# Attention over the sequence: the order of the searches for the largest logits, turned by LEAD and paired by length with the weighing steps

## The chip, the cores and the metric

The kernel runs on one core of one Trainium2 chip. The time is the device time of the whole launch in microseconds; smaller is better. Times before the change: 2765.39, 2770.46 and 2771.39 us, median 2770.46.

## What is computed

One decoder layer on x of shape (4, 1024, 256), everything in float32. Three residual blocks follow each other: a gated state-space scan, an attention over a short context (154 keys), and a block with causal attention over the sequence (1024 tokens, 16 heads of depth 16) followed by a mixture of eight experts of which each token uses two. The change touches only the causal attention:

```python
h = _ln(x, ln1_g, ln1_b)
q, k, v = h @ Wq + bq, h @ Wk + bk, h @ Wv + bv      # 16 heads of 16
scores = einsum('bhqd,bhkd->bhqk', q, k) / hd ** 0.5
scores = where(causal, scores, -inf)
attn = softmax(scores, axis=-1)
o = einsum('bhqk,bhkd->bhqd', attn, v)
a = o @ Wo + bo + x
```

## The kernel before

The attentions run on one core in one program whose order is written out by hand for TensorE, VectorE, ScalarE and GpSimd; only the DMA queue of SyncE is ordered by the framework.

*Layout.* A block is 512 query tokens (BLK), half of a batch. The 16 heads lie in four chunks (NCH = 4) of four heads; in a chunk each head takes 32 partitions (HP), of which 16 hold the head's depth. So a matmul over one head has 32 rows, and the four heads of a chunk lie on the four quarters of the rows. A *unit* is one chunk of one block: 8 units for each batch in the context attention and 8 for each batch in the sequence attention.

*Each unit has two halves.* First, `largest` finds the largest logit of each query, so that it can be subtracted ahead of the exponential. Its jobs put queries on the output partitions and keys on the columns: a job takes one tile j of 128 queries, a stretch of at most 512 keys from s0, and a `pair` of heads (0 or 1: heads 0 and 1 or heads 2 and 3, that is the lower or the upper half of the rows). For the causal attention this is `many` (L749): two matmuls into a PSUM tile `ps_max` (L755), for the stretch that ends at the diagonal an addition of the mask (L760), and a reduction to the negative maximum (L762). For the first block of a batch a unit has 8 jobs, of 128, 256, 384 and 512 keys, two of each. For the second block the queries see 640 to 1024 keys, cut into stretches of at most 512: ten jobs of 512, and two each of 384, 256 and 128; there the maxima of the two stretches go to `mpad` and `twice`.

When all searches of a unit are through, `put` (L764) takes the smaller of the two negative maxima (L766, only in second blocks), turns them with four transposes into the PSUM tile `shift` (L769), and adds them to the queries (L771, `qs`).

Second, `weighing` computes the logits again with keys on the output partitions and queries on the columns, for one tile kt of 128 keys and one pair of heads: two matmuls into `ps_exp` (L819), the exponential on ScalarE into `pt` (L821), and on the diagonal a triangle cut to zero on GpSimd (L825). Tiles of keys beyond the diagonal need fewer queries, so the columns are 512, 384, 256 and 128 for the four tiles of a first block, and 512 five times, then 384, 256 and 128 for the eight tiles of a second block. Each comes twice, for pair 0 and then pair 1. After pair 1, `weigh` (L786) multiplies earlier exponentials with the values (L793, `ps_o`).

*Buffers.* `ps_max` and `ps_exp` share three rotating PSUM tiles of two banks each (pool `a_pss`, tag `sc`). `pt` has five buffers, `mpad` two.

*Order.* The main loop walks over the steps of the weighing, unit by unit. After step k of unit u it runs the search jobs up to `upto`: those of unit u+1 in proportion, and LEAD = 5 jobs more. So the searches of a unit begin five jobs before the weighing of the unit ahead of it begins:

```python
upto.append(min(len(search), near + (far - near) * (k + 1) // n + LEAD))
```

`put` of a unit is called when two jobs of the next unit's searches have been issued. After that the loop takes `weigh` at every second step, and `fill` adds at most one job of other TensorE work per step: projections of coming blocks (`proj`, L702), values (`vals`, L715), transposes (`tp`, L689), the way back of finished attention (`back`, L840; `wo`, L859) and the router (L1061). GpSimd and VectorE do small jobs for these in the same order.

*The lines that the change touches* are the last ones of `largest`, where the jobs of the causal attention are put in a list: sorted by falling length, then by j, with pair 0 and pair 1 of each.

Of the kernel before, what the change touches and what calls it, by code (L numbers as in the profile page):

```python
# [27 lines left out]
LEAD = 5  # L28
# [5 lines left out]
BLK = 512  # L34
# [16 lines left out]
def decoder_layer(ctx: ExitStack, tc: tile.TileContext, out: bass.AP, a: dict):  # L51
# [52 lines left out]
    parts = dram.tile([TOPK * NTOK, D], F32, name="parts")  # L104
# [63 lines left out]
    with ExitStack() as ss:  # L168
# [55 lines left out]
        for lv in range(LV):  # L224
            r, h = slice(lv * 2 * NS, (lv + 1) * 2 * NS), 1 << lv
            for x in range(h):
                n = LC // h
# [340 lines left out]
        ready, jobs = prepare(0)  # L568
        for job in jobs:
            job()  # L570
        for blk in range(nblk):
            work = scan(blk, *ready)
            jobs = []
            if blk + 1 < nblk:
                ready, jobs = prepare(blk + 1)
# [27 lines left out]
    with ExitStack() as ss:  # L603
# [9 lines left out]
        def mm_tile(name):  # L613
            return ps_m.tile([P, BLK], F32, tag="mm", name=name)
# [24 lines left out]
        def turn(which, of_):  # L639
            turns[which] += 1  # L640
            return of_[(turns[which] - 1) % len(of_)]
# [83 lines left out]
        def largest(qT, kT, c, keys, diag, shifted):  # L725


            m = turn("m", mpads)
            n_all = [sum(x for _, x in keys) if diag is None else (diag + j + 1) * P for j in range(NJ)]
            jobs = []  # L730
            twice = small.tile([P, NJ, 4], F32, tag="twice", name="twice") if max(n_all) > BLK else None

            def few(j0, pair):

                n = n_all[j0]
                ps = ps_s.tile([P, 2, BLK], F32, tag="sc", name="ps_max")
                for j in range(j0, j0 + 2):
                    for i in range(2):
                        r = slice((2 * pair + i) * HP, (2 * pair + i + 1) * HP)
                        nc.tensor.matmul(  # L740
                            ps[:, i, (j - j0) * n : (j - j0 + 1) * n], qT[r, j * P : (j + 1) * P], kT[r, c, :n],
                            start=True, stop=True,
                        )
                nc.vector.tensor_reduce(  # L744
                    m[:, j0 : j0 + 2, 2 * pair : 2 * pair + 2, HD].rearrange("p j i -> p i j"),
                    ps[:, :, : 2 * n].rearrange("p i (j n) -> p i j n", n=n), AX.X, ALU.max, negate=True,
                )

            def many(j, s0, pair):  # L749
                n = n_all[j]  # L750
                s1 = min(n, s0 + BLK)
                ps = ps_s.tile([P, 2, BLK], F32, tag="sc", name="ps_max")
                for i in range(2):
                    r = slice((2 * pair + i) * HP, (2 * pair + i + 1) * HP)
                    nc.tensor.matmul(  # L755
                        ps[:, i, : s1 - s0], qT[r, j * P : (j + 1) * P], kT[r, c, s0:s1], start=True, stop=True
                    )
                if s1 == n:
                    x = ps[:, :, s1 - s0 - P : s1 - s0]
                    nc.vector.tensor_add(x, x, mask_qk.unsqueeze(1).to_broadcast([P, 2, P]))  # L760
                to = twice[:, j, 2 * pair : 2 * pair + 2] if s0 else m[:, j, 2 * pair : 2 * pair + 2, HD]
                nc.vector.tensor_reduce(to, ps[:, :, : s1 - s0], AX.X, ALU.max, negate=True)  # L762

            def put():  # L764
                if twice is not None:
                    nc.vector.tensor_tensor(m[:, :, :, HD], m[:, :, :, HD], twice, ALU.min)  # L766
                tp = mm_tile("shift")
                for j in range(NJ):
                    nc.tensor.transpose(tp[:, j * P : (j + 1) * P], m[:, j].rearrange("p g i -> p (g i)"), ident)  # L769
                shifted.append(ap_.tile([P, BLK], F32, tag="qs", name="qs", bufs=2))  # L770
                nc.vector.tensor_add(shifted[0], qT, tp)  # L771

            if diag is None:
                for j0 in range(0, NJ, 2):
                    for pair in (0, 1):
                        jobs.append(lambda j0=j0, pair=pair: few(j0, pair))
            else:
                parts = [(min(n - s0, BLK), j, s0) for j, n in enumerate(n_all) for s0 in range(0, n, BLK)]
                for _, j, s0 in sorted(parts, key=lambda x: (-x[0], x[1])):
                    for pair in (0, 1):  # L780
                        jobs.append(lambda j=j, s0=s0, pair=pair: many(j, s0, pair))
            return jobs, put

        waiting, ahead, behind = [], [], []
# [175 lines left out]
        def context(b):  # L960
# [36 lines left out]
            for half in range(T // BLK):  # L997
# [26 lines left out]
                for c in range(NCH):  # L1024
                    shifted = []
                    grp.units.append((
                        largest(qTs[c], kT, c, keys, None, shifted),
                        weighing(shifted, kT, vs, c, keys, None, oT, after if c == NCH - 1 else []),
                    ))
# [109 lines left out]
        def sequence(b):  # L1139
# [54 lines left out]
            for half, (v, qTs) in enumerate(halves):  # L1194
                blk = b * (T // BLK) + half
                xb = xs[:, blk * NJ : (blk + 1) * NJ, :]
                oT = [ap_.tile([P, BLK], F32, tag="oT", name="oT", bufs=5) for _ in range(NCH)]
                res = lazy(late, [P, 2, BLK], "res")
                after = joined(oT, res) + outputs(lambda: held["f"], res, v)
                after += route(blk, xb, v)  # L1200
                after.append(Job(lambda: reach("routed"), lag=0, mm=False))
                keys = [(x * P, P) for x in range(TB)]
                for c in range(NCH):
                    shifted = []
                    grp.units.append((
                        largest(qTs[c], kT, c, keys, half * NJ, shifted),
                        weighing(shifted, kT, vs, c, keys, half * NJ, oT, after if c == NCH - 1 else []),
                    ))
# [11 lines left out]
        for u, (_, jobs) in enumerate(units):  # L1220
            n, near, far = len(jobs), begins[min(u + 1, len(units))], begins[min(u + 2, len(units))]
# [92 lines left out]
    with ExitStack() as ss:  # L1314
# [50 lines left out]
        many = nc.values_load(flag[0:1, 0:1], min_val=0, max_val=P)  # L1365
        with tc.If(many == 0) as branch:
            with ExitStack() as sb:
# [24 lines left out]
                for n in range(NB):  # L1392
                    e = nc.sync.value_load(tab[0:1, 0, n : n + 1], min_val=0, max_val=E - 1)
                    s0 = nc.sync.value_load(tab[0:1, 1, n : n + 1], min_val=0, max_val=E * NTOK - MB)
# [95 lines left out]
```

## Time and profile before

| what | value |
|---|---|
| median of the timed runs | 2770.46 us |
| the profiled execution, its own time | 2737.4 us |
| its span, first to last instruction | 2735.6 us |
| mean granted TensorE clock | 0.927 |
| TensorE busy | 2423.8 us (89%) |
| VectorE busy | 1340.7 us (49%) |
| ScalarE busy | 1014.5 us (37%) |
| attention over the sequence, first to last weighing | 1116.8 to 2037 us, 920.2 us |
| experts | from about 2075 us on |

The profile is of one execution; its own time lies 33 us below the median of the timed runs. Times of instructions are read from that execution. In the lines of the profile a matmul in float32 counts as two records, since it takes two passes through the array, and a record that is written "32*128 32x512" has 32 rows, 128 columns of weights and streams 512 columns. PE is TensorE, PEld its loading of weights, DVE VectorE, ACT ScalarE, POOL GpSimd, SP SyncE. An arrow at the end of a line names what the idle time ahead of the instruction ended with. The busy time of PE is the time in which at least one matmul runs, whatever part of the array it uses.

### The profile page before, as it was taken

To read this page: it belongs to the slowest core of one execution; us is meant where nothing else is said; L and a number is where in the kernel's file an instruction comes from. 1 tells how busy PE (TensorE), PEld (TensorE's weight loads), DVE (VectorE), ACT (ScalarE), POOL (GpSimd) and SP (SyncE) were. 2 spreads that over 40 slices of the span, in tenths; PEclk is the share of its full clock that TensorE was granted. 3 is DMA by queue.
4 is the path that set the end of the run, shared out by engine and by line. 5 is a ranking of instruction groups with operands and counts; after the bars stand their busy time and mean duration, and the time that the engine had idled before them with its cause. 6 is when DMAs were issued, how large, how long until landed. Compare 5 with 4: busy or idle time off the path is not lost.

```text
span 2735.6 us, 36259 instructions
## 1 busy us (share of the span) xinstructions
PE 2423.8 (89%) x13582; PEld 1419.6 (52%) x13582; DVE 1340.7 (49%) x2718; ACT 1014.5 (37%) x1554; POOL 408.2 (15%) x640
## 2 busy tenths in 40 slices
PE   5999999996799999999999999899876999999990
PEld 2666665654344444433333333333335888888880
DVE  4767766566444345676666586566622111111113
ACT  2444334432355445535533544443331222222220
POOL 1110000000110001211312231231231111111110
PEclk9999999997789899999899998898987999999995
DMA  4596000001000000000001001010005555555545
GB/s 102 111 237 153 0 1 1 1 0 26 19 11 21 20 22 17 16 5 24 28 8 37 24 17 26 16 38 9 17 32 170 182 181 180 187 178 183 174 137 185
DMA packets 143601, 191.10 MB, mean 70 GB/s; under 512 B 34130, under 2 KB 114236, under 8 KB 143420
## 3 DMA queue, kind: packets, MB, share of 16 engines
q1 hardware_dynamic: 121628, 131.42, 15.6%
q0 software_dynamic: 15264, 51.00, 7.2%
q10 hardware_dynamic: 6528, 6.29, 0.7%
q8 instruction: 110, 1.80, 0.3%
q14 instruction: 71, 0.58, 0.1%
HBM read 116.03 MB, written 61.24 MB: 65 GB/s over the span
## 4 chain that ended last, share of the span: by engine, by line
PE 56%; issue 24%; DVE 10%; POOL 4%; ACT 3%; DMA 2%; SPq 1%; POOLq 0%; DVEq 0%; ACTq 0%
PE ps_exp L819 12%; PE ps_o L793 7%; PE ps_max L755 6%; PE proj L702 3%; PE ps_xz L310 3%; PE ps_a L327 3%; POOL parts L1381 3%; PE wo L859 2%; PE tp L689 2%; PE z L441 2%; PE ps_o L548 2%; PE ps_max L740 2%; PE vals L715 2%; PE shift L769 1%; PE tp_wt L419 1%
## 5 line engine op out<-in xcount | busy, mean ns | idle before, releaser
L821 ACT ACTIVATE pt<-ps_exp 128x1024 f32<-128x1024 f32 (+4 forms) x512 | 438.1, 861 | 539.1 <-PE ps_exp L819 443.2
L819 PE MATMUL ps_exp<-qs,kT 32*128 32x512 f32 (+4 forms) x2048 | 510.3, 590 | 6.4 <-DVE twice L762 1.9
L755 PE MATMUL ps_max<-kT,qa 32*128 32x512 f32 (+3 forms) x1536 | 363.9, 564 | 13.3 <-ACT pt L821 4.7
L1306 PE MATMUL ps<-hT,w 128*128 128x256 f32 x1248 | 288.3, 384 | 25.2 <-ACT mid L1307 23.5
L762 DVE TENSOR_REDUCE mpad<-ps_max 128x2 f32<-128x1024 f32 (+3 forms) x256 | 261.2, 1024 | 85.1 <-PE ps_max L755 77.9
L1307 ACT ACTIVATE mid<-ps,bias 128x256 f32<-128x256 f32 x312 | 139.4, 473 | 436.8 <-DMA bias<-b1s 257.3
L1312 PE MATMUL ps<-w,mid 128*128 128x256 f32 x1248 | 287.9, 379 | 0.0
L819 PEld LDWEIGHTS ps_exp<-qs,kT 32*128 32x128 f32 (+1 forms) x2048 | 150.1, 183 | 236.5 <-issue 132.3
L1306 PEld LDWEIGHTS ps<-hT,w 128*128 128x128 f32 x1248 | 232.7, 191 | 74.5 <-ACT mid L1307 38.8
L1312 PEld LDWEIGHTS ps<-w,mid 128*128 128x128 f32 x1248 | 234.2, 190 | 30.3
L793 PE MATMUL ps_o<-pt,vs 128*32 128x512 f32 (+4 forms) x2048 | 247.1, 552 | 1.6 <-ACT oT L801 1.2
L760 DVE TENSOR_TENSOR ps_max<-ps_max,mask_qk 128x256 f32<-128x256 f32 x256 | 109.8, 429 | 156.4 <-PE ps_max L755 96.7
L744 DVE TENSOR_REDUCE mpad<-ps_max 128x4 f32<-128x616 f32 x128 | 101.6, 799 | 169.3 <-PE ps_exp L819 113.2
L825 POOL TENSOR_SCALAR_AFFINE_SELECT pt<-pt 128x256 f32<-128x256 f32 x256 | 104.3, 408 | 511.8 <-ACT pt L821 510.6
L1379 DVE TENSOR_TENSOR y<-ps,last 128x256 f32<-128x256 f32 x78 | 33.1, 425 | 294.7 <-PE ps L1312 294.7
L755 PEld LDWEIGHTS ps_max<-kT,qa 32*128 32x128 f32 x1536 | 124.1, 194 | 72.3 <-ACT pt L821 37.4
L1381 POOL DMA_INDIRECT parts<-y,to x78 | 75.8, 972 | 525.0 <-DVE y L1379 521.1
L310 PE MATMUL ps_xz<-xnT,w_in 128*128 128x512 f32 x256 | 125.0, 605 | 0.6 <-ACT xnT L302 0.6
L327 PE MATMUL ps_a<-w,w_a 128*128 128x512 f32 x256 | 121.1, 615 | 0.0
L1406 DVE CAST to<-xr 128x2 int32<-128x2 f32 x39 | 6.6, 169 | 228.8 <-DMA parts<-y,to 201.6
L793 PEld LDWEIGHTS ps_o<-pt,vs 128*32 128x32 f32 (+1 forms) x2048 | 41.9, 110 | 145.0 <-issue 112.3
L740 PE MATMUL ps_max<-kT,qa 32*128 32x154 f32 x1024 | 110.7, 337 | 4.9 <-DVE mpad L744 3.2
(265 smaller groups left out, 3150.6 us busy)
## 6 DMA issues: line engine op xcount, KB each, us to landing
w<-in_L_ffn_e_w_dram SPq DMA_DIRECT2D x78, 1024.0 KB, 5.9
routed<-zero POOLq DMA_DIRECT2D x16, 2080.0 KB, 64.5
xr<-routed SPq DMA_DIRECT2D x39, 260.0 KB, 4.2
qa<-close SPq DMA_DIRECT2D x256, 32.0 KB, 1.9
last<-in_L_ffn_e_b_dram SPq DMA_DIRECT2D x39, 128.0 KB, 5.2
xs<-in_x_dram SPq DMA_DIRECT2D x4, 1024.0 KB, 8.7
kT<-close SPq DMA_DIRECT2D x128, 32.0 KB, 1.9
plain<-row SPq DMA_DIRECT2D x8, 512.0 KB, 3.1
```

Of the source, the lines that this page charges most:

```text
L310: nc.tensor.matmul(ps, w_in[:, k, c * P : (c + 1) * P], xnT[:, k, :], start=k == 0, stop=k == 1)
L327: nc.tensor.matmul(ps, w_a[:, k, c * P : (c + 1) * P], w[:, k, :], start=k == 0, stop=k == 3)
L740: nc.tensor.matmul(ps[:, i, (j - j0) * n : (j - j0 + 1) * n], qT[r, j * P : (j + 1) * P], kT[r, c, :n], start=True, stop=True,)
L755: nc.tensor.matmul(ps[:, i, : s1 - s0], qT[r, j * P : (j + 1) * P], kT[r, c, s0:s1], start=True, stop=True)
L762: nc.vector.tensor_reduce(to, ps[:, :, : s1 - s0], AX.X, ALU.max, negate=True)
L793: nc.tensor.matmul(o[0][g * HP : (g + 1) * HP, off:], vs[:n, kt, (4 * c + g) * HV : (4 * c + g) * HV + HP], pts[g // 2][:n, g % 2, off:], ...
L819: nc.tensor.matmul(ps[:n, i, off:], kT[r, c, k0 : k0 + n], shifted[0][r, off:], start=True, stop=True)
L821: nc.scalar.activation(pt[:n, :, off:], ps[:n, :, off:], AF.Exp, scale=HD**-0.5)
L1306: nc.tensor.matmul(ps, w1[:, k, f * P : (f + 1) * P], hT[:, k, :], start=k == 0, stop=k == 1)
L1307: nc.scalar.activation(mid[:, f, :], ps, AF.Gelu, bias=bias[:, f : f + 1])
L1312: nc.tensor.matmul(ps, mid[:, f, j * P : (j + 1) * P], w2[:, f, :], start=f == 0, stop=f == FF // P - 1)
L1381: nc.gpsimd.indirect_dma_start(out=parts, out_offset=bass.IndirectOffsetOnAxis(ap=to[:, j : j + 1], axis=0), in_=y[:, j, :], in_offset=Non ...
```

## The change

The list of search jobs of a unit of the causal attention is built in another order. It is still sorted by falling length and then by j, now with pair 1 ahead of pair 0, and then turned in a circle: the job at place i is the one at place i - LEAD of the sorted list. With LEAD = 5 a unit of eight jobs begins with the last five of the sorted list (384, 256, 256, 128, 128), and ends with its first three (512, 512, 384); a unit of sixteen begins with 384, 256, 256, 128, 128 and ends with ten of 512 and one of 384.

```diff
             else:
-                parts = [(min(n - s0, BLK), j, s0) for j, n in enumerate(n_all) for s0 in range(0, n, BLK)]
-                for _, j, s0 in sorted(parts, key=lambda x: (-x[0], x[1])):
-                    for pair in (0, 1):
-                        jobs.append(lambda j=j, s0=s0, pair=pair: many(j, s0, pair))
+
+
+                parts = [(min(n - s0, BLK), j, s0, p) for j, n in enumerate(n_all) for s0 in range(0, n, BLK) for p in (1, 0)]
+                parts.sort(key=lambda x: (-x[0], x[1]))
+                for i in range(len(parts)):
+                    _, j, s0, pair = parts[(i - LEAD) % len(parts)]
+                    jobs.append(lambda j=j, s0=s0, pair=pair: many(j, s0, pair))
             return jobs, put
```

The number of jobs, their contents and the points of the main loop at which they are issued stay as they are. This is how the matmuls stand on TensorE in the built programs, from the start of the weighing of the second unit of the first batch (columns and count of matmuls at the end of a row); lines behind L775 move by three in the changed kernel:

```
before                                        after
L819 ps_exp 128x512 x2                        L822 ps_exp 128x512 x2
L755 ps_max 128x256 x2                        L755 ps_max 128x512 x2
L819 ps_exp 128x512 x2                        L822 ps_exp 128x512 x2
L755 ps_max 128x128 x2                        L755 ps_max 128x512 x2
L793 ps_o 32x128 x4                           L796 ps_o 32x128 x4
L819 ps_exp 128x384 x2                        L822 ps_exp 128x384 x2
L755 ps_max 128x128 x2                        L755 ps_max 128x384 x2
L840 back 128x128 x4                          L843 back 128x128 x4
L819 ps_exp 128x384 x2                        L822 ps_exp 128x384 x2
L755 ps_max 128x512 x2 (next unit's)          L755 ps_max 128x384 x2 (next unit's)
L793 ps_o 32x512 x4                           L796 ps_o 32x512 x4
L819 ps_exp 128x256 x2                        L822 ps_exp 128x256 x2
L755 ps_max 128x512 x2                        L755 ps_max 128x256 x2
L769 shift 128x128 x4                         L769 shift 128x128 x4
L819 ps_exp 128x256 x2                        L822 ps_exp 128x256 x2
L755 ps_max 128x384 x2                        L755 ps_max 128x256 x2
L793 ps_o 32x384 x4                           L796 ps_o 32x384 x4
L819 ps_exp 128x128 x2                        L822 ps_exp 128x128 x2
L755 ps_max 128x384 x2                        L755 ps_max 128x128 x2
```

## Prediction

> **What bounds the kernel now.** I read the page first (busy shares, slices), then the windows of the stage that the change touches, then its timeline on TensorE, the groups by shape, and the waits. Terms: a *unit* is one chunk c of four heads over one half of a batch; E is one weighing step's two ps_exp matmuls, S one search job's two ps_max matmuls, W the four ps_o matmuls. While unit u runs its steps k = 0, 1, ..., the searches of unit u+1 run beside them.
>
> The page and the stage (attention over the sequence, from its first E to its last):
>
> ```profile
> PE 2423.8 (89%) x13582; PEld 1419.6 (52%) x13582; DVE 1340.7 (49%) x2718; ACT 1014.5 (37%) x1554; POOL 408.2 (15%) x640
> ...
> 1116.80:2037.00 920.20, 851.62 (x5502) 341.04 (x5502) 588.45 (x1184) 407.39 (x573) 228.57 (x427) 0.93 0.08 21
> ```
>
> The second line's columns are length, then busy time of PE, PEld, DVE, ACT and POOL, then the clock. PE is busy 852 of 920 us, DVE 588, ACT 407: TensorE is the bound, but a busy PE can hold a short matmul beside a long one. The timeline of PE shows that (start, length):
>
> ```profile
> 1161.87 0.59 PE L819 MATMUL ps_exp<-qs,kT 32*128 32x384 f32 x2
> 1161.88 0.70 PE L755 MATMUL ps_max<-kT,qa 32*128 32x512 f32 x2
> 1162.30 0.49 PE L819 MATMUL ps_exp<-qs,kT 32*128 32x384 f32 x2
> 1162.42 0.59 PE L755 MATMUL ps_max<-kT,qa 32*128 32x512 f32 x2
> 1162.94 1.06 PE L793 MATMUL ps_o<-pt,vs 128*32 128x512 f32 x8
> 1163.94 0.48 PE L819 MATMUL ps_exp<-qs,kT 32*128 32x256 f32 x2
> 1163.95 0.70 PE L755 MATMUL ps_max<-kT,qa 32*128 32x512 f32 x2
> 1164.26 0.38 PE L819 MATMUL ps_exp<-qs,kT 32*128 32x256 f32 x2
> 1164.48 0.59 PE L755 MATMUL ps_max<-kT,qa 32*128 32x512 f32 x2
> 1165.01 0.66 PE L769 MATMUL shift<-ident,mpad 128*128 128x128 f32 x4
> ...
> 1167.45 0.38 PE L819 MATMUL ps_exp<-qs,kT 32*128 32x128 f32 x2
> ...
> 1167.66 0.28 PE L819 MATMUL ps_exp<-qs,kT 32*128 32x128 f32 x2
> ```
>
> E and S start 0.01 us apart, on different quarters of the rows, and run together. Each matmul is two passes; the passes start 0.53 (512 columns), 0.43 (384), 0.32 (256) and 0.21 us (128) apart. So a step takes twice that for the *longer* of its two: 1.07, 0.85, 0.64, 0.42 us; E of 256 beside S of 512 costs 1.07 (1163.94 to 1165.01). W takes 1.00 at 512 columns (1162.94 to 1163.94).
>
> What can hold a step back is in the groups by shape and in this stretch of the timeline:
>
> ```profile
> L762 DVE TENSOR_REDUCE mpad<-ps_max 128x2 f32<-128x1024 f32 x156 | 189.8, 1223 | 81.6 <-PE ps_max L755 77.9 <-PE ps_exp L819 2.5
> L760 DVE TENSOR_TENSOR ps_max<-ps_max,mask_qk 128x256 f32<-128x256 f32 x243 | 104.2, 429 | 151.1 <-PE ps_max L755 95.4 <-PE ps_exp L819 49.2 <-ACT pt L821 3.0
> L821 ACT ACTIVATE pt<-ps_exp 128x1024 f32<-128x1024 f32 x192 | 195.1, 1023 | 198.1 <-PE ps_exp L819 129.7 <-PE ps_max L755 66.6 <-POOL row L1046 1.3
> ...
> 1589.83 0.59 PE L819 MATMUL ps_exp<-qs,kT 32*128 32x384 f32 x2
> ...
> 1590.70 0.91 PE L819 MATMUL ps_exp<-qs,kT 32*128 32x384 f32 x4
> 1590.85 1.67 ACT L821 ACTIVATE pt<-ps_exp 128x768 f32<-128x768 f32 x2 [0.20 <-PE ps_exp L819]
> ...
> 1591.71 1.13 PE L755 MATMUL ps_max<-kT,qa 32*128 32x512 f32 x4
> ```
>
> The third pair of lines: E and S take turns in three PSUM buffers (tag sc), so S of step k+1 needs the buffer that exp of E(k) empties, and E(k+2) the one that DVE empties of S(k). E(2) starts at 1589.83, E(3) at 1590.70, but S(3) only at 1591.71, 1.88 us after E(2). Exp starts 0.17 us after its E is through and lasts 1.02, 0.81, 0.60 or 0.38 us (groups of L821 by shape), so S(k+1) starts no sooner than 2.29, 1.86, 1.44 or 1.00 us after E(k) of 512, 384, 256, 128. Other PE work between k and k+1 (*fill*: transposes 0.59 us, proj, wo, vals, router 1.9 us) hides it.
>
> **The change part by part.** No instruction is added or removed; POOL and ACT keep their orders, SP moves two stores of plain by eight issues or fewer, which nobody waits for. Searches keep their places among steps, W and fill; only their lengths trade places. Before, S at step k was five jobs ahead in a list of falling length, so E 512,512,384,384,256,256,128,128 met S 256,128,128,512,512,384,384,256. Now it meets its own length. S also still sits on the row quarters that E of its step leaves free.
>
> *Ceiling.* Columns of the longer of the two: an 8-step unit beside 8 searches 3456, then 2560; 16 beside 16: 8064, then 6656. A column costs (1.07-0.42)/384 = 1.7 ns. Twelve of each kind: 12 x (896 + 1408) x 1.7 ns = 47 us, if nothing but PE counted. It does not, so I go by pairs of steps (k even, k+1, then W), without fill and W, at full clock.
>
> *16 beside 16 (12 units).* (0,1), (2,3): 512s in both, unchanged. (4,5), (6,7), (8,9): S of the second step was 384, 256, 128 and is 512. Where no long fill stands between, the pair ends at 2.29 plus S: 3.14, 2.93, 2.71 before, 3.36 after. Such pairs in the trace: 7, 5 and 7 of 12. That is +0.13, +0.18, +0.37 per unit. After a long fill, S(k+2) starts 0.22 late (2.29 against 1.07 + 1.00 of W); a short S hid that at k = 6, 8, 10, behind 5, 7, 5 of 12 long fills: +0.31. (10,11): 1.86 + 1.07 becomes 1.86 + 0.85: -0.22. (12,13) holds the shift: S ends at 0.64 instead of 1.07; then mask 0.43, reduce 0.69, min 0.18 and 0.2 of hand-over put the transposes at about 2.15 instead of 2.55, and step 13 is 0.64 instead of 1.07: -0.85. (14,15): E 128 beside S 512 twice, 2.14, becomes 1.42 without fill (1.00 + 0.42) and 0.84 with: -1.1 on average. Sum -1.18; x12 = -14.2 us.
>
> *8 beside 8 (12 units), all masked.* (0,1): 2.71 becomes 3.36 in 4 of 12, with a short fill +0.5 once: +0.25. (2,3): -0.22, but where a long fill before makes S(2) late (5 of 12) +0.17: -0.06. (4,5), with the shift, which here waits for nothing: 2.52 becomes 2.08, -0.45. (6,7): 2.40, 2.07, 1.50 (no, short, long fill; 2, 6, 4 of 12) becomes about 1.56, 0.97, 0.84: -0.91; the 1.56 holds a wait of 0.7 for DVE, whose queue is mask, reduce, mask, reduce with the qs addition (0.68) among them. Sum -1.17. In the first unit of each batch DVE is already about full (1116.8 to 1132.0: 13.2 of 15.2 us), so I count it at nothing: 8 x -1.17 = -9.4 us.
>
> *8 beside 16 (4 units)*: DVE sets the pace with the same work in both, 0. *16 beside 8 (3)*: equal sums, -0.6 in all. *Half clock*: 5 of the 12 (14,15) pairs ran so; a saving doubles there, -3 for what DVE leaves of it. *Against*: DVE's small jobs (bn_stats 0.42, reciprocals, additions) stand ahead of masks that are now waited for sooner: +4.
>
> Total -23 us. The profiled execution took 2737.4 us (span 2735.6), 33 below the median of 2770.46; I subtract the same 23 from the median: 2747.5 us, 0.8%.
>
> **Two rules of the skill against rows.** DVE's rows: a masked search costs 0.43 + 0.43 to 1.22 us plus two hand-overs; a pair of 128s 1.84, against PE's 0.84 and a W of 0.36 to 0.57. The Trainium skill, "TensorEngine Tiling (Array Packing)", PSUM Bottleneck, says that tiling speeds up the matmuls but not the emptying of PSUM, which may become the limit. Taken as the rule, every masked step goes at DVE's pace, the 8-step units win nothing and the 16-step units lose most of (14,15): about -2 us. By the rows DVE was idle 332 of 920 us, and W with a fill of 0.59 to 1.9 us (10 of 12 such pairs) covers most of it; I take the rows.
>
> The clock:
>
> ```profile
> PE shift L769 <- DVE mpad L766: 24.8, 16, 2.0
> ...
> 1526.20:1529.60 3.40, 1.42 (x12) 0.59 (x12) 2.48 (x7) 0.94 (x2) 1.09 (x2) 1.00 0.00 0
> 1529.60:1533.00 3.40, 3.40 (x22) 0.95 (x24) 2.61 (x6) 0.60 (x1) 0.73 (x2) 0.50 0.00 0
> ```
>
> The first line: TensorE waited 1.55 us on average for the min ahead of the shift. The windows: 3.4 us with PE busy for 1.42 were followed by 3.4 us at clock 0.50. The skill's "TensorE: Matmul & The Clock Gate" (Why this matters for your kernels) warns only of idle gaps above about 3 us; by it no clock is at stake, by the row a 2 us wait in a thin stretch can cost 1.7 us. The change leaves that wait near 1.5 us but thins the work round it: bounds 0 and 12 x 1.7 = +20; I take 0, as a wait of 1.42 us at 1257 drew no half clock, and keep +20 for the range.
>
> **The rivals.**
> 1. *DVE's pace* (above): the short steps give nothing back, -2 us, 2768. For: the mask and reduce of short steps take over twice PE's time. Against: fill and W.
> 2. *Slower: long pairs wait for exp.* The long steps that now all stand together pay 0.22 to 0.65 each through the three buffers: +0.99 per 16-step unit, +0.42 per 8-step unit, 12 of each, +17; with half-clock windows as above +8: 2787 to 2796. It decides if the short pairs give back less than 1 and 0.4 us per unit.
> 3. *Nearly the whole ceiling*: fills fall where they hide the waits, -40, 2730.
> 4. *The change doesn't pair equal lengths*: excluded; in the built program E 512 stands before S 512, E 128 before S 128, except beside 8 or 16 unequal steps.
>
> **How the numbers follow.** Forecast 0.62 (own range 2735 to 2762); rival 3 0.14; rival 1 0.10; rival 2 0.14. What a measurement can tell from no change is 0.2%, 5.5 us. Faster: 0.62 + 0.14 + 0.02 of rival 1 = 0.78; same 0.08; slower 0.14. The range leaves out most of rival 2 and the end of rival 3: 2726 to 2775.
>
> **What would show it.** After: pairs (14,15) and (6,7) shorter by about 1 us, 512-512 pairs without fill 3.36; L755's wait for ACT pt (4.7 us in 13 times) grows; the shift's wait stays near 1.5 us each; the stage loses about 23 of 920 us, DVE's busy 588 unchanged. Wrong if pairs of 128 take 1.8 and more, or half clock grows by over 20 us.

## The result, and the profile after

| kernel | timed runs | median us | range us | mean granted clock |
|---|---|---|---|---|
| before (first series) | 4 | 2770.93 | 2765.39 to 2776.06 | |
| changed (first series) | 4 | 2731.41 | 2724.77 to 2733.19 | 0.921 to 0.924 |
| before, once more (second series) | 22 | 2772.14 | 2739.30 to 2782.18 | 0.909 to 0.927 |
| changed, once more (second series) | 6 | 2733.74 | 2732.43 to 2739.24 | 0.920 to 0.923 |

The change makes the kernel faster: ratio 0.9853, 95% interval 0.9828 to 0.9879, some 40 us. In the second series it is 0.9891 (0.9849 to 0.9933), with medians 38 us apart; ratios leave out runs more than 1.5% above the fastest of their kernel, eleven of the 52 runs of the kernel before that this one was taken against, so it gives some 30 us. The forecast was 23 us (2747.5). Its range, 2726 to 2775, holds the 2731.4, but the narrower 2735 to 2762 of the forecast itself does not.

The changed kernel's profiled execution took 2732.85 us. The line of its page, and the whole stage (columns as before the change: length, busy PE, PEld, DVE, ACT, POOL, clock). The window runs from the first E to 20 us behind the last W, as does the window of 920.2 us shown before the change: there the last W ends at 2017.3 and not at 2037.

```profile
PE 2414.8 (88%) x13582; PEld 1431.2 (52%) x13582; DVE 1341.0 (49%) x2718; ACT 1014.7 (37%) x1554; POOL 408.8 (15%) x640
...
1124.90:2032.20 907.30, 833.39 (x5503) 347.80 (x5502) 591.02 (x1183) 407.33 (x573) 228.57 (x427) 0.92 0.08 22
```

Work and instructions are the same, DVE is as busy as before (588 and 591), the stage is 13 us shorter than the 920.2 shown before the change. That is a third of what the timed runs say, so the profile shown there was not a typical one: at 2737 us and clock 0.927 it is at the quick end of what that kernel does. A second trace of it, 2773.02 us at clock 0.913, stands below beside the changed kernel, split at the batches. The kernel before, second trace:

```profile
1123.80:1359.10 235.30, 223.91 (x1371) 88.51 (x1370) 146.93 (x273) 102.70 (x144) 48.24 (x94) 0.88 0.06 17
...
1834.90:2051.80 216.90, 199.08 (x1289) 76.79 (x1286) 132.82 (x273) 89.01 (x122) 53.90 (x105) 0.88 0.05 16
1123.80:2051.80 928.00, 868.62 (x5464) 343.10 (x5464) 582.61 (x1160) 406.01 (x570) 220.19 (x419) 0.90 0.07 20
```

Changed:

```profile
1124.90:1341.00 216.10, 203.88 (x1372) 83.93 (x1371) 146.42 (x273) 102.23 (x144) 48.25 (x94) 0.94 0.07 18
...
1796.10:2011.90 215.80, 196.22 (x1289) 78.05 (x1285) 133.67 (x273) 89.71 (x122) 53.85 (x104) 0.87 0.05 17
1124.90:2011.90 887.00, 821.33 (x5464) 339.87 (x5463) 584.44 (x1158) 405.57 (x570) 219.77 (x418) 0.92 0.07 21
```

Lines are first batch, last batch and all four up to the last W. Against this trace the stage is 41.0 us shorter, and the clock is to be read with it: 0.88 against 0.94 in the first batch. The first trace of before had 219.7 us at 0.95 there. So part of the gain is fewer microseconds at half clock, that is with a granted clock of 0.50 in the clock records; in the stage these records know only 0.50 and full clock.

*How much each part is.* The two traces of the kernel before hold 119.5 and 182.0 us of half clock between the first and the last E and differ by 27.6 us in length: 0.44 us for each microsecond of half clock (an estimate). With that price taken off, and units grouped by what runs beside what (8/16: an eight-step unit beside the sixteen searches of the next unit):

| units | forecast us | before (two traces) | changed | measured us |
|---|---|---|---|---|
| 16/16 (12) | -14.2 | 428.3, 427.9 | 418.5 | -9.6 |
| 8/8, but the first of a batch (8) | -9.4 | 135.6, 135.5 | 127.4 | -8.2 |
| first of a batch (4) | 0 | 61.5, 61.5 | 61.8 | +0.3 |
| 8/16 (4) | 0 | 101.7, 101.8 | 101.0 | -0.8 |
| 16/8 (3), last | -0.6 | 119.2, 119.7 | 118.2 | -1.3 |
| small jobs of DVE | +4 | | in the rows | |
| sum at equal clock | -20.2 | | | -19.6 |
| half clock | -3 | | 133.1 us of it | -21.6 against the second trace, +6.0 against the first |

The timed runs give the same split without any trace. A fit of time against clock over 74 runs of the kernel before and 10 of the changed one puts the changed kernel 19.4 us lower at equal clock (standard error 0.8); at a clock of 0.921 two runs of before took 2751.96 and 2752.68, four of the changed kernel 2732.7 to 2733.3. The remaining 19 us of the 38 between the medians are clock: 0.913 or 0.914 against 0.921.

*The pairs.* The timeline of PE in a masked eight-step unit of the changed kernel (unit 2 of the first batch, counted from 0; start and length):

```profile
1171.55 0.49 PE L822 MATMUL ps_exp<-qs,kT 32*128 32x256 f32 x2
1171.58 0.49 PE L755 MATMUL ps_max<-kT,qa 32*128 32x256 f32 x2
...
1173.63 0.85 PE L796 MATMUL ps_o<-pt,vs 128*32 128x384 f32 x8
1174.42 0.38 PE L822 MATMUL ps_exp<-qs,kT 32*128 32x128 f32 x2
1174.43 0.38 PE L755 MATMUL ps_max<-kT,qa 32*128 32x128 f32 x2
1174.63 0.28 PE L822 MATMUL ps_exp<-qs,kT 32*128 32x128 f32 x2
1174.64 0.28 PE L755 MATMUL ps_max<-kT,qa 32*128 32x128 f32 x2
1174.85 0.66 PE L689 MATMUL tp<-ident,on 128*128 128x128 f32 x4
1175.44 0.38 PE L822 MATMUL ps_exp<-qs,kT 32*128 32x128 f32 x2
```

Equal lengths begin 0.01 to 0.03 us apart, and the matmuls behind them start when both are through; the step of 128 columns takes 0.43 us (1174.42 to 1174.85). Pairs of steps without the time of W and fill, in us at full clock (8/8 with the first units of a batch):

| pair | before | changed | |
|---|---|---|---|
| 16/16 (8,9), no, short, long fill | 2.73, 2.14, 2.12 | 3.37, 2.78, 2.37 | dearer |
| 16/16 (6,7) | 2.94, 2.36, 2.21 | 3.37, 2.78, 2.34 | dearer |
| 16/16 (12,13), with the shift, median | 4.22 | 3.44 | cheaper |
| 16/16 (14,15), no fill, fill | 2.09, 2.14 | 1.45, 0.88 | cheaper |
| 8/8 (0,1), no, short, long fill | 2.73, 2.12, 2.12 | 3.37, 2.63, 2.51 | dearer |
| 8/8 (6,7) | 2.40, 2.07, 1.50 | 1.74, 0.92, 0.91 | cheaper |

The wait views hardly show the dearer pairs: PE's wait at L755 for ACT pt went from 4.7 us in 13 times to

```profile
PE ps_max L755 <- ACT pt L824: 5.9, 16, 0.6
```

They are seen only in the timeline, here a pair (8,9) without fill of the changed kernel:

```profile
1254.50 0.70 PE L822 MATMUL ps_exp<-qs,kT 32*128 32x512 f32 x2
1254.51 0.70 PE L755 MATMUL ps_max<-kT,qa 32*128 32x512 f32 x2
...
1255.47 1.02 PE L822 MATMUL ps_exp<-qs,kT 32*128 32x512 f32 x4
...
1255.73 1.94 ACT L824 ACTIVATE pt<-ps_exp 128x1024 f32<-128x1024 f32 x2 [2.43 <-PE ps_max L755]
...
1256.81 1.13 PE L755 MATMUL ps_max<-kT,qa 32*128 32x512 f32 x4 [0.31 <-ACT pt L824]
```

S(9) starts at 1256.81, 2.31 after E(8), when the first exponential is through. In the meantime E(9) runs alone: the wait turns a shared step into two, and only 0.31 us of it is idle.

### The profile page after: what moved, and what is told of

It reads as the page before. It is cut to its first block, busy times and chain, and to the rows that moved or that the text cites. A ratio compares the mean times of both kernels' runs of the same rounds, so it can differ in the third digit from the quotient of the medians.

```text
span 2731.2 us, 36229 instructions
## 1 busy us (share of the span) xinstructions
PE 2414.8 (88%) x13582; PEld 1431.2 (52%) x13582; DVE 1341.0 (49%) x2718; ACT 1014.7 (37%) x1554; POOL 408.8 (15%) x640
## 4 chain that ended last, share of the span: by engine, by line
PE 55%; issue 23%; DVE 12%; POOL 4%; ACT 3%; DMA 2%; SPq 0%; POOLq 0%; DVEq 0%; ACTq 0%
PE ps_exp L822 13%; PE ps_o L796 7%; PE ps_max L755 4%; PE ps_xz L310 3%; PE proj L702 3%; PE ps_a L327 3%; POOL parts L1384 3%; PE wo L862 2%; PE tp L689 2%; PE z L441 2%; PE ps_max L740 2%; PE ps_o L548 2%; DVE mpad L762 2%; PE shift L769 2%; PE tp_wt L419 1%
## 5 line engine op out<-in xcount | busy, mean ns | idle before, releaser
L822 PE MATMUL ps_exp<-qs,kT 32*128 32x512 f32 (+4 forms) x2048 | 525.5, 604 | 9.4 <-DVE mpad L762 7.3
L755 PE MATMUL ps_max<-kT,qa 32*128 32x512 f32 (+3 forms) x1536 | 361.3, 564 | 8.7 <-ACT pt L824 5.9
L755 PEld LDWEIGHTS ps_max<-kT,qa 32*128 32x128 f32 x1536 | 124.7, 196 | 63.7 <-ACT pt L824 36.2
L327 PE MATMUL ps_a<-w,w_a 128*128 128x512 f32 x256 | 128.6, 648 | 0.0
L740 PE MATMUL ps_max<-kT,qa 32*128 32x154 f32 x1024 | 117.2, 352 | 3.0 <-ACT pt L824 1.2
```

The source lines that it names most:

```text
L327: nc.tensor.matmul(ps, w_a[:, k, c * P : (c + 1) * P], w[:, k, :], start=k == 0, stop=k == 3)
L740: nc.tensor.matmul(ps[:, i, (j - j0) * n : (j - j0 + 1) * n], qT[r, j * P : (j + 1) * P], kT[r, c, :n], start=True, stop=True,)
L755: nc.tensor.matmul(ps[:, i, : s1 - s0], qT[r, j * P : (j + 1) * P], kT[r, c, s0:s1], start=True, stop=True)
L822: nc.tensor.matmul(ps[:n, i, off:], kT[r, c, k0 : k0 + n], shifted[0][r, off:], start=True, stop=True)
```

## The experiments

### Each half of the change alone

Against the changed kernel; the other of the two has 16 in place of 8:

```diff
-                parts.sort(key=lambda x: (-x[0], x[1]))
+                turned = len(parts) == 8
+                parts.sort(key=lambda x: (-x[0], x[1]) if turned else (-x[0], x[1], x[2], x[3]))
...
-                    _, j, s0, pair = parts[(i - LEAD) % len(parts)]
+                    _, j, s0, pair = parts[(i - LEAD) % len(parts) if turned else i]
```

> The kernel before once more, to see how far two series of the same program lie apart and how far one profile lies from the timed runs. Every theory: 0 us, within 0.2% (5.5 us). If the first profile of the kernel before (2737.4 us, 33 us below its median) was only a quick execution, this profile lies nearer 2770 us, and its sequence stage is longer than 920 us; if the profiled execution is always quicker, it lies near 2737 again.

> The changed kernel once more. Theory A (pairs of steps: the long pairs lose 0.2 to 0.7 us each to the wait for the exponential, the short pairs gain 0.4 to 1.1 us): -23 us, and the pairs as in the first profile after. Theory B (nearly the whole ceiling of columns, something else gains too): -40 us, as the first comparison showed. Theory C (the 40 us are partly scatter between executions): between -15 and -30 us.

> Only the units of eight searches are turned and reordered; those of sixteen keep the old order. Theory A: -9 us (8 units at -1.17), at most -14 if the first unit of each batch gains as well. Theory B (columns): 12 x 896 x 1.7 ns = -18 us. Rival 1 (VectorE's pace, since all searches here are masked): 0.

> Only the units of sixteen searches are turned and reordered; those of eight keep the old order. Theory A: -14 us (12 units at -1.18). Theory B (columns): 12 x 1408 x 1.7 ns = -29 us. If the two parts are independent, this and the run with only the units of eight add up to the whole change.

The kernel before against itself: 1.0020 (0.9987 to 1.0052). Its runs lie between 2736 and 2782 us, at clocks from 0.927 down to 0.908, and the first profile was at the quick end. Eight alone: 2755.28 us, 0.9967 (0.9943 to 0.9991); sixteen alone: 2743.40, 0.9921 (0.9892 to 0.9950). By the medians -16 and -28, together more than the -37 of the whole against the same 52 runs; by the same fit at equal clock -6.0 and -17.1, against forecasts of -9.4 and -14.2, with 19.4 for the whole. So the small sum was near, and what exceeds it is clock. But the two halves do not test the two terms of the forecast, since the first five searches of a unit run in the unit ahead of it. At equal half clock the 8/8 units are as long with eight alone as before (135.5 us) and the 16/16 units lose 7.1; with sixteen alone 8/8 loses 8.2 and 16/16 5.5. The last pairs (6,7) of eight-step units fell from 1.93 us to 1.45 with eight alone, to 1.53 with sixteen alone, and to 1.05 with both.

### Equal lengths on the same rows

```diff
-                parts = [(min(n - s0, BLK), j, s0, p) for j, n in enumerate(n_all) for s0 in range(0, n, BLK) for p in (1, 0)]
+                parts = [(min(n - s0, BLK), j, s0, p) for j, n in enumerate(n_all) for s0 in range(0, n, BLK) for p in (0, 1)]
```

> The changed kernel with pair 0 ahead of pair 1 in the sorted list: the same lengths stand side by side, but search and weighing step use the same two quarters of the rows. Theory A (the gain is that two matmuls on different row quarters run together, so a step takes the longer): the two now run one after the other, up to (12 x 2560 + 12 x 6656) columns x 1.7 ns = +189 us on the changed kernel for the equal units alone; waits for VectorE and ScalarE swallow part of it, so +100 to +190, 2830 to 2920. Rival: the rows do not matter and only the order of lengths does: 0, within 0.3%.

2994.82 us, 261 us above the changed kernel. The timeline of PE (first batch), then the window of the whole stage of this kernel:

```profile
1188.63 1.13 PE L822 MATMUL ps_exp<-qs,kT 32*128 32x512 f32 x4
1189.44 2.26 PE L755 MATMUL ps_max<-kT,qa 32*128 32x512 f32 x8
```

```profile
1124.20:2272.70 1148.50, 1091.30 (x5464) 464.77 (x5464) 586.05 (x1158) 411.62 (x570) 220.02 (x418) 0.79 0.06 16
```

E, then S: they no longer share the time. That the lengths match is worth nothing where the rows do; the gain is row quarters that work together. The cost exceeds the range expected because the clock fell as well, from 0.92 to 0.79, with the same 5464 records and a PE that is 95% busy: 480 us of half clock in the stage instead of 133, at 0.44 us each some 150 of the 261 (an estimate). A busy PE does not hold the clock up here.

### Does the wait at the shift draw half clock?

The filler, in `put`, for units of sixteen searches:

```diff
                 tp = mm_tile("shift")
+                for _ in range(6 if twice is not None else 0):
+                    nc.tensor.transpose(tp[:, :P], ident, ident)
```

> The kernel before, plus six idle transposes of the identity (about 1.0 us by the 0.66 us of four shift transposes) ahead of the four shift transposes of each sixteen-search unit, where TensorE waits 1.55 us on average for the minimum. They write the PSUM tile that the shift transposes overwrite; the output is the same. Theory K (a 3.4 us window in which TensorE is busy for under about 58% is followed by half clock): the windows at the shift, busy 0.42 to 0.58 of 3.4 us, come to 0.7 and more, the half-clock windows that start at steps 12 and 13 go, and the kernel gets faster by added work: -10 to -25 us, median 2745 to 2760. Theory O (the half clock there has another cause, for instance how many rows or columns are in use): 0 to +5 us.

> The changed kernel plus the same six idle transposes ahead of the four shift transposes of each sixteen-search unit. Theory K1 (the changed kernel owes its higher clock to the same windows at the shift that the filler repaired in the kernel before; few half-clock windows start there any more): the filler gains little, 0 to -12 us on the changed kernel, 2720 to 2733; the two together are then far less than the sum of -37 and -38 us. Theory K2 (the change raised the clock at other places): the filler gains its full -30 to -38 us here too, 2695 to 2703. Theory O: 0 to +5 us.

Idle work added to the kernel *before* makes it as fast as the changed one: 2725.42 us, 0.9874 (0.9821 to 0.9927), about 35 us by this ratio, at clocks of 0.925 to 0.930. Windows of 3.41 us round a shift of the kernel before in its second trace (the second line holds the wait; the column after POOL is the clock):

```profile
1308.35:1311.77 3.42, 3.17 (x24) 0.74 (x20) 1.87 (x4) 1.94 (x3) 1.99 (x7) 1.00 0.00 0
1311.77:1315.18 3.41, 1.68 (x16) 0.89 (x20) 2.37 (x5) 0.01 (x2) 0.97 (x2) 1.00 0.00 0
1315.18:1345.90 30.72, 30.72 (x128) 12.48 (x122) 12.09 (x49) 9.94 (x14) 5.09 (x8) 0.50 0.01 4
1345.90:1349.31 3.41, 3.41 (x24) 0.87 (x20) 1.66 (x2) 2.21 (x3) 0.00 (x0) 1.00 0.02 7
```

Windows round the same shift with the filler:

```profile
1296.82:1300.23 3.41, 3.41 (x30) 1.25 (x24) 1.69 (x4) 2.24 (x3) 1.14 (x5) 1.00 0.02 5
1300.23:1303.65 3.42, 2.24 (x17) 1.25 (x18) 2.58 (x4) 0.60 (x1) 1.97 (x6) 1.00 0.00 0
1303.65:1307.06 3.41, 3.41 (x33) 1.53 (x31) 2.51 (x4) 0.98 (x2) 0.81 (x2) 1.00 0.01 2
```

A wait of 2 us was followed by nine windows, 30.7 us, at clock 0.50; with 0.88 us of transposes in the wait, none. With the filler no half clock starts at a shift of any of the twelve 16/16 units (five in the second trace without it). With the price of half clock taken off, those units take 428.2 us, against 427.9: nothing but the clock has changed in them. After the stage this kernel is another 8 us shorter than the second trace, and by the fit its six runs lie 9 us lower at equal clock; why is open, so some 8 of the 35 us are not shown to come from the filler.

In the changed kernel the same filler brought 2725.85 us, 8 below the changed kernel's median, as the first theory there expected: the change has already dealt with part of what the filler mends. With the filler both kernels have 99.0 us of half clock in the stage, down from 182.0 (second trace; 119.5 in the first) and from 133.1; half clock begins at three of the twelve shifts of the changed kernel's trace, at five in the second and at three in the first of the kernel before. The change does not do it by a shorter wait (waits of the changed kernel):

```profile
PE shift L769 <- DVE mpad L766: 27.6, 16, 2.3
```

27.6 us in 16 times, 24.8 before. What differs is how much runs around it (last section).

### The shift a step later

```diff
-                if min(begins[put[0] + 1] + 2, len(search)) <= found[0]:
+                if found[0] == begins[put[0] + 1] + 2 and len(units[put[0]][0][0]) == 16:
+                    some = True
+                elif min(begins[put[0] + 1] + 2, len(search)) <= found[0]:
...
-                    some = True
+                    some = some or found[0] != begins[put[0]] + 3
```

> The changed kernel with the minimum and the shift transposes of sixteen-search units issued one step later, behind the step that follows, so that TensorE has a pair of matmuls of 256 columns to run while VectorE works on the last searches; all fills stay at their steps. Theory K: the wait of 27.6 us in 16 transposes shrinks to under 15, the thin window goes, -10 to -20 us. Theory D (VectorE's chain sets the pace there; its two further searches stand ahead of the minimum): the wait stays near 1.5 us each, 0 to +5 us.

> The kernel before with the same move of the shift by a step; here the step that goes ahead of it is a search of 512 columns (1.07 us of TensorE, and a masked or plain reduction of 1.22 us on VectorE ahead of the minimum). Theory K: -10 to -25 us, more than in the changed kernel since more half clock starts there. Theory D: 0 to +5 us.

Theory K missed, and the loss is larger than the 5 us that theory D allowed: 2751.42 us in the changed kernel (18 slower than its median), 2778.31 in the one before (1.0081, 1.0053 to 1.0109). The wait, in the changed kernel with the later shift:

```profile
PE shift L769 <- DVE mpad L766: 28.9, 16, 3.1
```

It moved with the shift: VectorE had the additional searches ahead of the minimum, as theory D said, and the clock fell to 0.907 to 0.920. By the fit this kernel lies 19.2 us below the kernel before at equal clock, as the changed one does (19.4): all of its 18 us are clock. A wait behind a chain of DVE is not filled by a step that lengthens that chain; idle work that no other engine touches does fill it.

### Does VectorE set the pace?

```diff
-                if s1 == n:
+                if s1 == n and s0 > BLK:
```

s0 is 0 or 512 and BLK is 512, so the addition is left out everywhere.

> The changed kernel without the addition of the causal mask in the searches, so that the maxima run over later keys of the diagonal tile too; 243 additions of 0.43 us on VectorE are gone, everything else stays. Theory A (VectorE costs time only at the shift, in the units beside unequal steps and in unfilled short pairs): the shift comes about 0.5 us sooner in 12 units (-6), the four units of eight steps beside sixteen searches lose 3 us each (-12), the unfilled last pairs of eight-search units 2 x 0.7: -15 to -25 us, and up to -15 more if fewer thin windows draw half clock. Rival 1 (VectorE's pace sets every short step): about half of the 104 us of additions comes back, -50 us or more. If VectorE never binds: 0.

2697.48 us, 0.9761 (0.9719 to 0.9803), 36 below the changed kernel, at clocks of 0.923 to 0.927. 101 us of DVE's work are gone from the stage, and the wait at the shift is shorter (window, then line of the waits):

```profile
1124.90:1985.40 860.50, 815.30 (x5464) 337.88 (x5463) 483.52 (x915) 404.55 (x570) 219.95 (x418) 0.93 0.08 22
```

```profile
PE shift L769 <- DVE mpad L766: 16.1, 16, 1.4
```

The stage lost 26.5 us; the 16/16 pairs with the shift fell from a median of 3.44 to 2.90, while (14,15) stayed at 1.03 on average (1.04) and (6,7) of 8/8 at 0.99 (1.05). So rival 1 is refuted for the short steps: without the mask they are no faster. VectorE costs time at the shift (16/16 units -10.5 us in all, at equal half clock) and in eight-step units: -3.9 in 8/8, -3.7 in 8/16, where the expectation had 12, and -4.0 in the first ones of a batch. There the forecast had counted DVE as full (13.2 of 15.2 us), but added lengths that overlap; the window of that unit, 1116.8 to 1132.0, has DVE busy for 12.06.

### What the long pairs wait for

This kernel leaves out half of the exponentials of the sequence stage: the second head of a pair gets a copy of the first one's weights from GpSimd.

```diff
-                nc.scalar.activation(pt[:n, :, off:], ps[:n, :, off:], AF.Exp, scale=HD**-0.5)
+                if diag is None:
+                    nc.scalar.activation(pt[:n, :, off:], ps[:n, :, off:], AF.Exp, scale=HD**-0.5)
+                else:
+                    nc.scalar.activation(pt[:n, 0, off:], ps[:n, 0, off:], AF.Exp, scale=HD**-0.5)
+                    nc.gpsimd.tensor_copy(pt[:n, 1, off:], pt[:n, 0, off:])
```

> The changed kernel with the exponential of the causal attention taken of one head of each pair only (the second head gets a copy of the first's weights from GpSimd, so that half of the heads are not computed): ScalarE empties the PSUM tile of a 512-column step in about 0.60 instead of 1.02 us. Theory R (the long equal pairs wait through the three PSUM buffers for the exponential): 512 pairs without fill go from 3.37 to about 2.95 us, with a short fill from 2.78 to about 2.36, with a long one from 2.37 to 2.14; over 60 long pairs in sixteen-step units and 12 in eight-step units -20 to -30 us. Rival (the buffer that binds is the search's, which VectorE empties, or TensorE alone): those pairs stay within 0.1 us and the time within -5 to +5 us.

The timeline of the same pair (8,9) as above:

```profile
1248.78 0.70 PE L822 MATMUL ps_exp<-qs,kT 32*128 32x512 f32 x2
...
1249.75 1.02 PE L822 MATMUL ps_exp<-qs,kT 32*128 32x512 f32 x4
...
1250.01 0.60 ACT L827 ACTIVATE pt<-ps_exp 128x512 f32<-128x512 f32 x1 [2.47 <-PE ps_max L755]
...
1250.66 1.13 PE L755 MATMUL ps_max<-kT,qa 32*128 32x512 f32 x4
```

S(9) starts 1.88 us after E(8) instead of 2.31. The pairs (8,9) went to 2.94, 2.36 and 2.14 (no, short, long fill), as theory R said to 0.01 us: the ring's third buffer, held by the exponential, sets them. The time followed less: 2719.50 us, 14 below the changed kernel instead of 20 to 30. The 16/16 units gained 15.7 us at equal half clock, others lost 7 of it again, and half clock grew from 133 to 147 us. GpSimd's work in the stage doubled with the copies (220 to 411 us); whether that is where the 7 went is not shown.

### A version that beats both

The changed kernel without the mask addition, with the filler at the shift, and in `weigh`, where four `back` blocks follow each other:

```diff
                     behind.pop(0).do()
+                    idle = ps_s.tile([P, 2, BLK], F32, tag="sc", name="ps_idle")
+                    for _ in range(5 if any(x.soon for x in behind) else 0):
+                        nc.tensor.transpose(idle[:, 0, :P], ident, ident)
```

> The changed kernel without the mask addition in the searches, with six idle transposes ahead of the shift transposes of sixteen-search units, and with five idle transposes (about 0.8 us, into a free tile of the ring sc) after each of the first three of the four back blocks that run in a row at step 1 of every third unit of four, where TensorE waits 0.90 us for each next one. Measured so far: 2697.5 us without the mask addition alone; the filler at the shift alone gained about 8 us on the changed kernel. Theory K: the thin windows at step 1 of units 2 and 6 (busy 0.48 to 0.58 of 3.4 us where they draw half clock, eight such places in the sequence stage and eight in the context stage) go as well, another -5 to -20 us: 2672 to 2692. Theory O (idle matmuls only cost): 2697 to 2705, as the wait at the shift is now only 1.0 us and the idle tiles take their turn in the ring of three.

2633.25 us, 0.9548 (0.9500 to 0.9595): 64 us below the kernel without the mask addition, far beyond the 5 to 20 expected. Window of the stage:

```profile
1107.90:1923.70 815.80, 790.93 (x5635) 339.46 (x5635) 482.76 (x915) 404.16 (x570) 220.69 (x418) 1.00 0.08 23
```

171 records more than without fillers, and 44.7 us less. Clock 1.00 (rounded): 7 us of half clock are left of 123. The context attention ahead of it went from 413.6 to 394.3 us, its half clock from 90 to 52.

## Why the prediction was right, and where it was not

- *Bound, overlap, length of a step*: right. Steps take the longer of two on different row quarters; on the same rows the overlap is gone.
- *The sum*: -20.2 us without half clock, against -19.4 at equal clock. That they agree is in part luck. Two terms were off and cancelled: 16/16 units gave 9.6 instead of 14.2, and the +4 for DVE's small jobs was not seen as a cost of its own. The 14.2 counted twelve equal units. But in the third 16/16 unit of each batch the last five searches are those of the next batch's first unit (512, 512, 384, 384, 256 before the change), and in the last batch there are none. So E 128 met 384 and 256 there, or nothing, instead of 512 twice, and there was less to win: some 5 of the 14.2 us by the lengths of the steps (an estimate). In five of the other eight the last pair ran at full clock in both kernels and gained 0.64 us without fill and 1.25 with it, near the forecast.
- *The long pairs*: right in mechanism and size (3.36 forecast without fill, 3.37 measured). L755's wait for ACT pt grew as forecast, but by 1.2 us only: the cost sits in E running alone.
- *8/8*: (0,1) cost 0.42 instead of 0.25, (6,7) gained 0.88 (forecast 0.91). First units 0 and 8/16 nearly 0, as counted.
- *Half clock*: the step that failed, "-3 for what DVE leaves of it". It measured -19 by the timed runs. The range held all the same because it was wide, not because this was counted. The forecast looked at five (14,15) pairs of one trace that was itself at the quick end, and feared up to +20 at the shift instead of asking how full the array is. The 33 us between that profile and the median were a hint left unused: most runs of the kernel hold half clock which that trace did not show.
- *Rivals*: that nearly the whole ceiling of 47 us is won (2730) is the nearest number and the wrong reason, since at equal clock only 19.4 of 47 came. *DVE's pace* is refuted by the mask experiment and the pairs of 0.88. *Slower by the ring*: the ring costs what was said, the short pairs give back more.
- *The two rules*: the rows were right against "TensorEngine Tiling (Array Packing)"; with the clock, neither the page's gap of about 3 us nor the reading by busy time was the right measure.

Still open: how much of the 19 us is denser work and how much where the windows of the clock (last section) happen to lie. The kernel before shows both cases in itself (clock 0.908 to 0.927), the changed one in ten runs only 0.920 to 0.924. The traces speak for a small part of denser work: among all stretches of 3.41 us that lie at full clock, those too thin to keep it by the measure of the last section are 7.1% and 6.8% in the two traces of the kernel before, 6.2% in the changed kernel, and 3.8% in the kernel before with the filler.

## What to carry to other kernels

Where two streams of matmuls on different row quarters share TensorE, order them so that equal lengths meet, and count the pairs where a buffer makes one of them run alone, since a busy PE hides it. Before costing microseconds, look at the granted clock of more than one execution: 33 us between a profile and the median was half clock. A wait of 2 us that cannot be removed may be worth filling with idle full-array transposes: the kernel before with six of them per sixteen-search unit was as fast here as the reordered one.

## What the runs showed of the hardware that was not expected

Busy time does not tell what clock comes next; the filled part of the array does. The half-clock records of the stage are multiples of 3.41 us. For each such window I summed, over the matmul passes in it, columns x rows/128 x weight columns/128, and divided by the length (an estimate, since the ends of matmuls are modelled). A pass of 512 columns over 128x128 every 0.53 us is 966 per us. In the sequence stage of fourteen traces of this study, windows that lie wholly between the first E and the last W:

| window now | columns per us | windows | half clock in the next |
|---|---|---|---|
| full clock | 450 and more | 2797 | 0 |
| full clock | under 450 | 262 | 240 |
| half clock | 470 and more | 193 | 0 |
| half clock | 420 to 470 | 124 | 82 |
| half clock | under 420 | 323 | 322 |

Of the windows at full clock, the best cut by this measure leaves 21 on the wrong side; by PE's busy time it leaves 134, by columns x rows alone 109. One threshold fits both states in these traces, near 450, or 47% of the 966; but that is nearly all of the 483 that half clock can reach (half of 966). This fits how long half clock lasts: E and S of 512 together fill 128 rows and reach 957 per us (2 x 512 in 1.07 us), or 478 at half clock, enough; 512 beside 256 reaches 359 at half clock, and E alone, with 64 rows, 240. In the 30.7 us at half clock shown above, with PE busy throughout, the kernel before ran this:

```profile
1326.57 2.08 PE L819 MATMUL ps_exp<-qs,kT 32*128 32x512 f32 x4
1328.43 1.06 PE L755 MATMUL ps_max<-kT,qa 32*128 32x256 f32 x4
...
1332.18 1.22 PE L819 MATMUL ps_exp<-qs,kT 32*128 32x512 f32 x2
1332.20 0.80 PE L755 MATMUL ps_max<-kT,qa 32*128 32x128 f32 x4
```

Its windows hold 95 to 418 columns per us; the first with 513 ended it. At the shift of unit 5 of the first batch the window held 430 in the second trace of the kernel before (half clock followed), 522 in its first (none) and 554 in the changed kernel (none). The measure also fits the kernel with equal rows, the same passes on half of the array at a time: 140 of its 335 windows were at half clock, 39 of 258 in the changed kernel. The windows are not tied to the program: in its two traces the same shift of the kernel before fell into one window or was split over two, which fits that runs of one program lay up to 46 us apart. The Trainium skill, "TensorE: Matmul & The Clock Gate" (Part 1: The HAM clock gate), has such a free-running window of about 3.4 us, and the records here are multiples of 3.41; that the filled array tells the next clock and busy time does not is what these runs add.
